# Four layers on one core: layer 1's mixing takes each token's second expert result by a product of its own

## The chip, the core and the metric

The kernel runs on one core of a Trainium2 chip. The core has five engines that work side by side, each with its own queue of instructions in order: TensorE (PE; PEld is its loading of stationary operands), VectorE (DVE), ScalarE (ACT), GpSimd (POOL) and SyncE (SP). SP issues most DMA transfers, POOL those whose rows are picked by an index (gathers). The metric is the device time of one execution in microseconds (us); lower is better.

## The reference, cut to what matters

The input is 32 sequences of 64 tokens, 2,048 tokens of 512 numbers. Four layers follow one another, and each adds to its input: `x = x + ffn(cond(x))`. Layer 0 ends in a mixture of 7 experts, of which each token uses 2; layer 1 begins with a mixing and goes on to a mixture of 32 experts, of which each token uses 4:

```python
x = x + _L0_ffn_ref(_L0_cond_ref(x, ...), ...)
x = x + _L1_ffn_ref(_L1_cond_ref(x, itok_B_0_7, L1_cond_weights), ...)

def _L1_cond_ref(x, subjects, weights):
    w = weights[subjects]
    out = jnp.einsum('bct,bcd->bdt', x, w)
    return out
```

For each of the 32 sequences the mixing picks one of 8 matrices of 64 by 64 and multiplies the 64 rows of the sequence by it. The input of this mixing is layer 0's result. For one token that is a sum: what layer 0 had before its routed experts, plus gate 0 times the result of its first expert, plus gate 1 times that of its second. The same sum is also the residual to which layer 1's result is added later.

## The kernel before, in words

Tokens are handled in 16 tiles of 128 (`NT`); a tile holds two sequences. All values are float32, and the program runs a float32 product as two passes of PE.

Both mixtures are worked by one class, `Moe`. In a loop over the tiles it scores the experts of each token and gives every pair of token and expert a slot: 640 slots for each of layer 0's experts and 320 for each of layer 1's. `Moe.put` does this slot arithmetic for groups of 4, 4, 4, 2, 1 and 1 tiles, on DVE with small products on PE (`at`, `tok`). `Moe.run` then goes through the slots: it gathers the tokens' rows from DRAM (`xr`, five tiles of 128 for a pair of units), turns them on PE (`tp`, copied out by ACT and DVE in turn as `xT`), multiplies by the gate and up weights (`gu`, L943, four buffers), applies the activation (for layer 1 `ga` on DVE, `sg` on ACT, `ga` times `sg` on POOL, `up` and `hT` on DVE, L671 to L678), multiplies by the down weights (`y`, L962), and stores the result (`yo`) in a DRAM array `ys`. A unit is 320 slots, which for layer 1 is one expert; each expert brings 1.5 MB of weights (`wt`, three buffers), loaded through SP's queue. After each tile of 128 results, `run` calls a function that it was given (`per_tile`), so that other work can be issued beside the experts.

`Moe.run` returns `combined`, which the next layer uses to fetch a tile of tokens: for each of a token's `K` experts it gathers the result from `ys` by its slot (`g.gather`, L284, on POOL) and adds it, times its gate, on DVE (L1010).

Layer 1's mixing (in `layer1`, L1090 to L1113) is the loop that the change touches. `Bridge` has prepared, beside layer 0's experts, the 16 tiles of x without the routed experts (`bridge.x`) and for each tile a 128x128 matrix `bridge.weights[i]` with the two sequences' matrices on its diagonal. For each tile the loop calls `combined` with `K0 = 2`, so two gathers and two adds, and stores the sum to the DRAM array `xs` (named `x1`), from which layer 2 will read it. Then comes one product with the mixing matrix (`mm`, L1094), a copy to SBUF by ACT (`c`), a store of the rows that the experts will gather, four transpositions (`tp`, L1100), another copy by ACT (`cT`), eight passes for the router's scores (`rp`, L1105), and on DVE the choice of the four best experts, with `m.put` for every finished group. When the loop is done, the slot lists are complete (`stok`, L792), and the first gathers of `Moe.run` can be issued.

A scheduler sets the order of each engine's instructions when the program is built, from the order in which they are written and its own estimates of cost; instructions marked as kept in program order stay where they are written. The order within a queue is then fixed, and an engine that waits holds back all that stands behind it. A tile pool gives each name its number of buffers (`bufs`): a writer waits until the last reader of the buffer is done. The pool `w2` holds the weights of layer 2, among them `mu` (`sb_mu`), 4 MB that are loaded beside layer 1's experts by the generator `layer2_ahead`; `layer1` calls it as `beside` from `ahead`, for every tile of results from the 17th on.

Of the kernel before, what the change touches and what calls it, by code (L numbers as in the profile page):

```python
# [9 lines left out]
F32 = mybir.dt.float32  # L10
# [4 lines left out]
AF = mybir.ActivationFunctionType  # L15
ALU = mybir.AluOpType
# [4 lines left out]
P = 128  # L21
B, T, D = 32, 64, 512
NT = B * T // P
# [5 lines left out]
E0, K0, C0, V0 = 7, 2, 640, 24  # L29
# [151 lines left out]
class Prog:  # L181
# [35 lines left out]
    def results(self, pool):  # L217

        zero = pool.tile([P, D], F32, name="zero")
        self.nc.vector.memset(zero, 0.0)  # L220
        self.ys = {}
        todo = []
        for E, C, V in ((E0, C0, V0), (E1, C1, V1)):
            t = self.dram.tile([E * C + V * P, D], F32, name=f"ys{E}")
            todo += [(t, r) for r in range(E * C, E * C + V * P, 8 * P)]
            self.ys[E] = t

        def step():
            if todo:
                t, r = todo.pop(0)  # L230
                self.dma(
                    t[r : r + 8 * P, :].rearrange("(v p) d -> p v d", p=P),
                    zero.unsqueeze(1).to_broadcast([P, 8, D]),
                )

        return step
# [444 lines left out]
class Moe:  # L681
# [228 lines left out]
    def run(self, xs, per_tile):  # L910

        g, nc, tc, E, K, C = self.g, self.g.nc, self.g.tc, self.E, self.K, self.C
        units = E * C // UNIT
        with ExitStack() as ctx:
            sb = ctx.enter_context(tc.tile_pool(name=f"es{E}", bufs=3, reuse_waits="tile"))
# [108 lines left out]
        def add(x, yk, gate):  # L1024
            g.pin(nc.vector.scalar_tensor_tensor(x, yk, gate, x, ALU.mult, ALU.add))

        combined.fetch = fetch
        return combined


# [42 lines left out]
def layer1(g, bridge, combined, beside, w2):  # L1073
    tc, nc, a = g.tc, g.nc, g.a
    with ExitStack() as ctx:
        keep = ctx.enter_context(tc.tile_pool(name="l1keep", bufs=1, reuse_waits="tile"))
        g.constants(keep, "cst01")
        xs = g.stream("x1")
        m = Moe(g, ctx, keep, E1, K1, C1, V1, "w_e1", W1R, l1_expert, None, bias="b_d1")
        with ExitStack() as c1:  # L1080
            wp = c1.enter_context(tc.tile_pool(name="l1w", bufs=1, reuse_waits="tile"))
            sb = c1.enter_context(tc.tile_pool(name="l1sb", bufs=3, reuse_waits="tile"))
            ps = c1.enter_context(tc.tile_pool(name="l1ps", bufs=2, space=PSUM, reuse_waits="tile"))
            wr = g.load(wp, "w_r1")
            br = g.load_bcast(wp, "b_r1")
            bank, at = (ps.tile([P, 512], F32, name=k, tag=k, bufs=1) for k in ("tok", "at"))
            m.begin(sb, bank, at)

            groups = {3: 4, 7: 4, 11: 4, 13: 2, 14: 1, 15: 1}
            for i in range(NT):  # L1090
                x = combined(sb, i, 3, bridge.x[i])
                nc.sync.dma_start(out=xs[i * P : (i + 1) * P, :], in_=x)
                o = ps.tile([P, D], F32, name="mm", tag="mm")
                nc.tensor.matmul(o, bridge.weights[i], x, start=True, stop=True)  # L1094
                c = sb.tile([P, D], F32, name="c")
                nc.scalar.copy(c, o)
                nc.sync.dma_start(out=m.rows[i * P : (i + 1) * P, :], in_=c)
                tp = ps.tile([P, 4, P], F32, name="tp", tag="tp")
                for cc in range(4):
                    nc.tensor.transpose(tp[:, cc, :], c[:, cc * P : (cc + 1) * P], g.ident)  # L1100
                cT = sb.tile([P, 4, P], F32, name="cT", bufs=2)
                nc.scalar.copy(cT, tp)
                rp = ps.tile([P, E1], F32, name="rp", tag="rp")
                for cc in range(4):
                    nc.tensor.matmul(rp, cT[:, cc, :], wr[:, cc, :], start=cc == 0, stop=cc == 3)  # L1105
                lg = sb.tile([P, E1], F32, name="lg")
                nc.vector.tensor_tensor(lg, rp, br, ALU.add)
                m.choose(i, lg)
                for last in (i - 1, i) if i == NT - 1 else (i - 1,):
                    if last in groups:  # L1110
                        m.put(sb, last + 1 - groups[last], groups[last])
            for e in range(2):
                m.weights(e)  # L1113
            m.end(sb)
            bridge.close()
        m.ready(ctx)

        gates, vals = m.gates, m.vals
        nc.vector.tensor_tensor(
            gates, vals[:, :, 0:K1], vals[:, :, 0:1].to_broadcast([P, NT, K1]), ALU.subtract  # L1120
        )
        nc.scalar.activation(gates, gates, AF.Exp)
        tot = keep.tile([P, NT], F32, name="tot1")
        nc.vector.tensor_reduce(tot, gates, AX.X, ALU.add)
        nc.vector.reciprocal(tot, tot)
        nc.vector.tensor_tensor(gates, gates, tot.unsqueeze(2).to_broadcast([P, NT, K1]), ALU.mult)

        def ahead(sb, ps, i):
            if i >= NT:
                w2["sb"], w2["ps"] = sb, ps  # L1130
                next(beside, None)

        combined = m.run(xs, ahead)
        m.beyond()
        return combined
# [975 lines left out]
def program(tc, a):  # L2111
    with ExitStack() as ctx:
        g = Prog(tc, a, ctx)
        w3 = {}
        pool3 = ctx.enter_context(tc.tile_pool(name="w3", bufs=1))
        bridge, combined = layer0(g, w3, pool3)
        first = ctx.enter_context(tc.tile_pool(name="w2a", bufs=1, reuse_waits="tile"))
        with tc.tile_pool(name="w2", bufs=1, reuse_waits="tile") as pool:
            w2 = {"pool": pool}
            beside = layer2_ahead(g, first, pool, w2)  # L2120
            combined = layer1(g, bridge, combined, beside, w2)
            for _ in beside:
                pass
            xs, xb = layer2(g, w2, combined, first, w3)
        layer3(g, w3, xs, xb)
# [17 lines left out]
```

## Time and profile before

| what | value |
|---|---|
| time, median of 3 runs | 2753.23 us (2749.45 to 2755.63) |
| the profiled execution, its own time | 2775.78 us |
| span of the profiled execution | 2774.0 us |
| busy over the span: PE, DVE, POOL, ACT | 2569.8, 1413.0, 845.6, 722.7 us |
| layer 1's mixing, from its first gather to the end of `stok` | 644.2 to 742.3 us |
| layer 1's experts, until PE's last product for them | 743 to about 1236 us |

The profile is one execution recorded by the hardware. Positions are microseconds from the start of the span. A row of a group names the line, the engine, the operation, what it writes and reads, the number of instructions, their busy time in us and the mean of one in ns, and behind the last bar the idle time of the engine before them with what ended it. A row in order of time begins with the start and the length in us; in square brackets stand the idle time before it and its releaser. The granted clock is the share of full speed at which PE ran.

### The profile page before, as it was taken

To read this page: it belongs to the slowest core of one execution; us is meant where nothing else is said; L and a number is where in the kernel's file an instruction comes from. 1 tells how busy PE (TensorE), PEld (TensorE's weight loads), DVE (VectorE), ACT (ScalarE), POOL (GpSimd) and SP (SyncE) were. 2 spreads that over 40 slices of the span, in tenths; PEclk is the share of its full clock that TensorE was granted. 3 is DMA by queue.
4 is the path that set the end of the run, shared out by engine and by line. 5 is a ranking of instruction groups with operands and counts; after the bars stand their busy time and mean duration, and the time that the engine had idled before them with its cause. 6 is when DMAs were issued, how large, how long until landed. Compare 5 with 4: busy or idle time off the path is not lost.

```text
span 2774.0 us, 41860 instructions
## 1 busy us (share of the span) xinstructions
PE 2569.8 (93%) x16508; PEld 1650.9 (60%) x16523; DVE 1413.0 (51%) x3439; ACT 722.7 (26%) x1501; POOL 845.6 (30%) x904
## 2 busy tenths in 40 slices
PE   6999989996799999978899999999999999887778
PEld 5777765564565565646666666776666654444444
DVE  4666655733644444435554444455544326555656
ACT  2444420011211121101222222222222212444444
POOL 2222215514223223212222221222222018655550
PEclk9999999996699999998999999999999999888889
DMA  2333215446557875643000000110001024233330
GB/s 95 128 128 128 86 55 178 137 164 216 191 182 251 321 258 197 220 144 115 28 28 28 27 28 28 36 46 27 28 27 51 9 97 154 71 90 97 98 98 29
DMA packets 111633, 299.50 MB, mean 108 GB/s; under 512 B 21177, under 2 KB 21977, under 8 KB 104128
## 3 DMA queue, kind: packets, MB, share of 16 engines
q1 hardware_dynamic: 75792, 201.78, 20.4%
q0 software_dynamic: 35056, 89.13, 10.8%
q10 hardware_dynamic: 576, 5.77, 0.5%
q8 instruction: 134, 2.20, 0.3%
q14 instruction: 75, 0.61, 0.1%
HBM read 225.08 MB, written 87.56 MB: 113 GB/s over the span
## 4 chain that ended last, share of the span: by engine, by line
PE 48%; DVE 2%; issue 2%; another core or an unknown queue 1%; DMA 1%; ACT 1%; POOL 0%; SPq 0%; ACTq 0%; POOLq 0%; DVEq 0%
PE lp L1376 8%; PE out L1519 8%; PE zp L1453 8%; PE pp L1833 3%; PE hp L1485 3%; PE gp L1508 2%; PE y L2080 2%; PE yp L1321 2%; PE op L2058 2%; PE sp L2011 2%; PE pT L2033 2%; PE ep L1462 1%; PE kp L1984 1%; PE ap L1309 1%
## 5 line engine op out<-in xcount | busy, mean ns | idle before, releaser
L943 PE MATMUL gu<-xT,wt 128*128 128x320 f32 x1472 | 408.7, 434 | 0.0
L943 PEld LDWEIGHTS gu<-xT,wt 128*128 128x128 f32 x1472 | 278.8, 191 | 123.4 <-issue 16.8
L1376 PEld LDWEIGHTS lp<-xnT,sb_mu 128*128 128x128 f32 x2048 | 236.2, 194 | 8.6 <-issue 6.7
L962 PE MATMUL y<-wt,hT 128*128 128x512 f32 (+1 forms) x552 | 240.3, 608 | 0.4 <-DVE yo L971 0.4
L1376 PE MATMUL lp<-xnT,sb_mu 128*128 128x128 f32 x2048 | 239.2, 277 | 1.5 <-DVE xnT L256 0.8
L1519 PE MATMUL out<-sb_w,gT 128*128 128x512 f32 x512 | 233.9, 599 | 0.0
L1453 PE MATMUL zp<-sb_w,xnT 128*128 128x512 f32 x512 | 226.5, 592 | 0.0
L1512 DVE COPY gT<-gp 128x512 f32<-128x512 f32 x64 | 44.3, 692 | 235.8 <-PE gp L1508 235.4
L1453 PEld LDWEIGHTS zp<-sb_w,xnT 128*128 128x128 f32 x512 | 93.7, 190 | 104.7 <-issue 100.9
L284 POOL DMA_INDIRECT xr<-rows,stok x115 | 110.0, 956 | 150.8 <-PE tp L924 78.7
L1519 PEld LDWEIGHTS out<-sb_w,gT 128*128 128x128 f32 x512 | 93.5, 190 | 103.7 <-issue 95.4
L284 POOL DMA_INDIRECT yk<-ys,slot x96 | 99.6, 1038 | 133.1 <-SPq L823 65.8
L962 PEld LDWEIGHTS y<-wt,hT 128*128 128x128 f32 (+1 forms) x552 | 80.4, 172 | 99.1 <-issue 83.2
L677 POOL TENSOR_TENSOR ga<-ga,sg 128x320 f32<-128x320 f32 x64 | 55.0, 859 | 267.5 <-ACT sg L673 263.9
L1530 POOL TENSOR_TENSOR xt<-xt,bc_bias 128x512 f32<-128x512 f32 x16 | 20.3, 1267 | 360.0 <-DMA x<-xt 360.0
L1490 ACT ACTIVATE h<-hp 128x512 f32<-128x512 f32 x128 | 69.5, 595 | 214.5 <-PE hp L1485 214.4
L284 POOL DMA_INDIRECT kvt<-kv,gidx x96 | 93.5, 973 | 102.2 <-PE op L2058 75.8
L2018 DVE CUSTOM_DVE_ANT_0 s<-sp,mask 128x336 f32<-128x336 f32 x128 | 61.2, 504 | 120.9 <-PE sp L2011 35.5
L1414 POOL TENSOR_TENSOR eT<-eT,inv 128x512 f32<-128x512 f32 x64 | 71.2, 1114 | 152.4 <-DVE inv L1413 151.4
L284 POOL DMA_INDIRECT kvt<-newkv,oidx x96 | 96.6, 1006 | 31.8 <-issue 29.2
L673 ACT ACTIVATE sg<-ga 128x320 f32<-128x320 f32 x64 | 30.0, 469 | 279.0 <-DVE ga L671 275.2
L924 PEld LDWEIGHTS tp<-sb_cst,xr 128*128 128x128 f32 x460 | 54.4, 148 | 67.2 <-issue 36.4
(379 smaller groups left out, 4647.7 us busy)
## 6 DMA issues: line engine op xcount, KB each, us to landing
wt<-w_e SPq DMA_DIRECT2D x32, 1538.0 KB
ys<-yo SPq DMA_DIRECT2D x115, 256.0 KB
ys<-zero SPq DMA_DIRECT2D x10, 2048.0 KB
xt<-x SPq DMA_DIRECT2D x62, 256.0 KB
x<-xt SPq DMA_DIRECT2D x48, 256.0 KB
wt<-w_e SPq DMA_DIRECT2D x7, 1536.0 KB
bd<-b_d SPq DMA_DIRECT2D x32, 256.0 KB
sb_w<-w SPq DMA_DIRECT2D x5, 1024.0 KB
```

What stands on the lines that cost most here:

```text
L284: ins = self.nc.gpsimd.indirect_dma_start(out=out, out_offset=None, in_=src, in_offset=bass.IndirectOffsetOnAxis(ap=idx, axis=0), **kw)
L943: nc.tensor.matmul(o, wj[:, c, ic * P : (ic + 1) * P], xT[:, c, :], start=c == 0, stop=c == 3)
L962: nc.tensor.matmul(y[row : row + n, :], hTs[u][:, ic, col : col + n], wd[:, ic, :], start=ic == 0, stop=ic == 1,)
L1321: g.first(c, nc.tensor.matmul(yp, self.xT[:, c, :], w["w_2"][:, c, :], start=c == 0, stop=False))
L1376: g.first(e + c, nc.tensor.matmul(lp[:, e, :], w["mu"][:, c, (4 * q + e) * P : (4 * q + e + 1) * P], self.xnT[:, c, :], start=c == 0, stop ...
L1414: g.pin(nc.gpsimd.tensor_tensor(e3, e3, inv.unsqueeze(2).to_broadcast([P, 8, T]), ALU.mult))
L1453: g.first(c, nc.tensor.matmul(zp, self.xnT[:, c, :], w["w1"][:, c, cols], start=c == 0, stop=c == 3))
L1485: g.first(e + b, nc.tensor.matmul(hp[:, b, e, :], self.ews[q][r, e, :], self.z[q][r, e * P : (e + 1) * P], start=True, stop=True))
L1490: g.pin(nc.scalar.activation(self.hs[q][b], hp[:, b], AF.Gelu))
L1519: g.first(e, nc.tensor.matmul(self.out, self.gTs[q][:, e, :], w["w2"][:, 4 * q + e, :], start=q + e == 0, stop=q + e == 6 and q == 3))
L1833: nc.tensor.matmul(pp, xT[i][:, c, :], (w["w_kv3"] if z else wq)[:, c, :], start=c == 0, stop=c == 3)
L2018: nc.vector.tensor_tensor_reduce(p, sps[j], self.masks[2 * i + half], -0.0625, 3.0e38, ALU.add, ALU.min, m)
```

## The change

The first result of each token is handled as before: gathered, multiplied by its gate and added to `bridge.x` on DVE. The product with the mixing matrix takes this partial sum. The second result is not added to it. Its rows are gathered (`y1of`) and are themselves the moving operand of a second product, whose stationary operand is the mixing matrix with row p multiplied by the gate of token p (`wbdg`, made by ACT). Both products accumulate in the same PSUM tile, so that the mixing sees the same sum as before. Nothing is rounded differently by type; all of it is float32.

The residual, which needs the whole sum, gets its second part later. The partial sums of all 16 tiles stay in SBUF (`x1in`, in the place that `sb_mu` takes afterwards). In `ahead`, beside the experts, for each of the first 16 tiles of results the second result of token tile `i` is gathered once more (two buffers), multiplied by its gate, added to `x1in` on DVE, and the sum is stored to `xs`. The stores to `xs` thus move from the mixing loop to the expert stage, and 16 gathers are added there; the mixing loop keeps its 32.

```diff
+        def result(pool, i, k, bufs):
+
+            yk = pool.tile([P, D], F32, name=f"y{k}of", bufs=bufs)
+            g.gather(yk, self.ys, self.slot[:, i, k : k + 1])
+            return yk, self.gates[:, i, k : k + 1]
+
+        combined.fetch, combined.result = fetch, result
@@ layer1
+        xk = w2["pool"].tile([P, NT, D], F32, name="x1in", tag="sb_mu")
+        results = combined.result
@@
             for i in range(NT):
-                x = combined(sb, i, 3, bridge.x[i])
-                nc.sync.dma_start(out=xs[i * P : (i + 1) * P, :], in_=x)
+                x, wbd = xk[:, i], bridge.weights[i]
                 o = ps.tile([P, D], F32, name="mm", tag="mm")
-                nc.tensor.matmul(o, bridge.weights[i], x, start=True, stop=True)
+                for k in range(K0):
+                    y, gate = results(sb, i, k, 3)
+                    if k == 0:
+                        nc.vector.scalar_tensor_tensor(x, y, gate, bridge.x[i], ALU.mult, ALU.add)
+                        nc.tensor.matmul(o, wbd, x, start=True, stop=False)
+                    else:
+
+                        wg = sb.tile([P, P], F32, name="wbdg", bufs=2)
+                        nc.scalar.activation(wg, wbd, AF.Copy, scale=gate)
+                        nc.tensor.matmul(o, wg, y, start=False, stop=True)
                 c = sb.tile([P, D], F32, name="c")
@@ ahead
             if i >= NT:
                 w2["sb"], w2["ps"] = sb, ps
                 next(beside, None)
+                return
+            y, gate = results(sb, i, 1, 2)
+            nc.vector.scalar_tensor_tensor(xk[:, i], y, gate, xk[:, i], ALU.mult, ALU.add)
+            nc.sync.dma_start(out=xs[i * P : (i + 1) * P, :], in_=xk[:, i])
```

More of the change, by code (lines that the diff above doesn't have):

```diff
@@ L1025, in add @@
             g.pin(nc.vector.scalar_tensor_tensor(x, yk, gate, x, ALU.mult, ALU.add))
-        combined.fetch = fetch
+        def result(pool, i, k, bufs):
[3 more added lines that the diff above has]
+        combined.fetch, combined.result = fetch, result
         return combined
```

## The prediction

> **What bounds the kernel now.** I read the page first, then stretches of 5 us around the edited loop, the groups of that loop, the rows in order of time where the next stage starts, and the waits of the expert stage. On the page: TensorE (PE) is busy 93% of the span, and its granted clock (PEclk, tenths, one digit per 69 us) falls to 6 only in slices 10 and 11, 624 to 763 us. That is where layer 1's mixing lies.
>
> ```profile
> PE 2569.8 (93%) x16508; PEld 1650.9 (60%) x16523; DVE 1413.0 (51%) x3439; ACT 722.7 (26%) x1501; POOL 845.6 (30%) x904
> ...
> PEclk9999999996699999998999999999999999888889
> ```
>
> Stretches of that stage (stretch, length, busy us of PE, PEld, DVE, ACT, POOL with instruction counts, granted clock, DMA share, GB/s):
>
> ```profile
> 655.00:660.00 5.00, 3.94 (x22) 2.78 (x21) 1.91 (x3) 1.76 (x4) 3.91 (x4) 0.84 0.95 285
> 660.00:665.00 5.00, 4.03 (x19) 3.06 (x20) 3.61 (x9) 1.75 (x3) 4.08 (x4) 0.84 0.94 315
> ...
> 675.00:680.00 5.00, 5.00 (x20) 3.97 (x19) 1.81 (x6) 1.75 (x3) 2.70 (x3) 0.50 0.96 311
> 680.00:685.00 5.00, 5.00 (x16) 3.50 (x16) 3.27 (x13) 0.98 (x2) 0.00 (x0) 0.50 0.37 131
> 685.00:690.00 5.00, 5.00 (x21) 4.00 (x20) 1.91 (x7) 1.74 (x4) 1.92 (x2) 0.50 0.53 186
> ...
> 705.00:710.00 5.00, 5.00 (x33) 3.53 (x32) 3.85 (x14) 3.23 (x6) 2.71 (x3) 1.00 0.99 320
> ```
>
> So the stage has three limits in turn: transfers until 680 (DMA share 0.95), then PE, busy without a gap from 675 to 695 but at half clock, then VectorE (DVE) with the slot arithmetic. Groups from 640 to 740 us:
>
> ```profile
> L284 POOL DMA_INDIRECT yk<-ys,slot x32 | 35.3, 1104 | 94.8 <-SPq L823 65.8 <-DVE vals L758 12.8 <-issue 7.6
> L1094 PE MATMUL mm<-xt,wbd 128*128 128x512 f32 x32 | 25.8, 902 | 17.1 <-DVE xt L1010 14.9 <-issue 1.6 <-DVE row L739 0.6
> L1010 DVE SCALAR_TENSOR_TENSOR xt<-yk,gates,xt 128x512 f32<-128x512 f32 x32 | 23.8, 745 | 16.0 <-DMA yk<-ys,slot 15.4 <-issue 0.5
> L1105 PE MATMUL rp<-sb_w_r,cT 128*128 128x32 f32 x128 | 23.0, 337 | 8.9 <-ACT cT L1102 6.8 <-DVE lg L1107 1.7 <-issue 0.5
> ```
>
> The experts follow. From 760 on PE is full, at clock 1.00, so any microsecond that it waits there lengthens the run. Rows at the seam (start, length, what):
>
> ```profile
> 743.10 0.94 POOL L284 DMA_INDIRECT xr<-rows,stok  x1 [34.57 <-DVE stok L792]
> ...
> 759.07 0.87 POOL L677 TENSOR_TENSOR ga<-ga,sg 128x320 f32<-128x320 f32 x1
> ```
> ```profile
> 746.51 1.09 PE L924 MATMUL tp<-sb_cst,xr 128*128 128x128 f32 x4 [4.67 <-DMA xr<-rows,stok]
> ...
> 776.67 1.09 PE L924 MATMUL tp<-sb_cst,xr 128*128 128x128 f32 x8
> ```
> ```profile
> 762.86 0.55 DVE L675 TENSOR_SCALAR up<-gu,wt 128x320 f32<-128x320 f32 x1 [1.15 <-PE gu L943]
> ...
> 775.84 0.69 DVE L256 COPY xT<-tp 128x512 f32<-128x512 f32 x1 [0.25 <-PE tp L924]
> ```
>
> A gather issued at 743.10 is used at 746.51: 3.4 us; the next four take 3.6 to 3.9, so I use 3.5. And the stage shows once what a held-up DVE does to PE, around 1045, where DVE waited for a POOL operation (waits, 1030 to 1055: us, times, longest):
>
> ```profile
> DVE cn L1174 <- POOL cn L308: 3.3, 1, 3.3
> ...
> PE tp L924 <- DVE xT L256: 2.4, 1, 2.4
> ```
>
> 3.3 us on DVE became 2.4 us of idle PE: the fourth turned tile of a pair needs the second one's evacuation by DVE.
>
> **The change, part by part. A: the mixing loop.** Gone: 16 of 32 adds of L1010 (16 x 0.745 = 11.9 us of DVE) and 16 stores of 256 KB, which leave SP's queue and a quarter of the loop's 64 transfers. Added: 16 products of two passes, and 16 small scalings on ScalarE (ACT). No row shows that scaling; ACT's 128x64 operation takes 0.26 us and its 128x320 copy 0.55, so 0.3 each, 4.8 in all, on an engine busy under 2 of 5 us in each stretch above: nothing, and 4.8 if that cover were gone. VectorE's add is no longer between the second gather and PE.
>
> The product is not small. Its two passes take 2.05 us at half clock (664.11) and 1.05 at full (666.81), the four transposes 1.06 and 0.60, the eight router passes 1.9 and 0.97. PE per tile: 5.0 (half) or 2.6 (full) before; 7.1 or 3.65 after. At full clock throughout: 16 x 3.65 = 58.4, plus the slot products (5.7 + 4.1 + 3.7 in the groups, at a mean clock near 0.65, so 8.8 at full) = 67.2. PE also waits once: in the built order DVE does three of the remaining adds between the first group's counting and the counts that PE needs, and their gathers, issued about 669 to 673 behind the earlier ones (1.25 us each), land 3.5 later: 3.1 us. The first product starts at 648.6 (landing 647.8, one add), so the last router product ends at 648.6 + 67.2 + 3.1 = 718.9 instead of 730.4: -11.5 us. The 12 us from there to the finished slot lists (742.35) are unchanged.
>
> What the clock does is not shown for this mix. In stretches of 1 us it falls at 670.3, in a wait of 5.3 us, and comes back at 704.2 only, though PE was nearly always busy between; it came back within 4 us where products and transposes ran back to back (650.3 to 656.3). The new sequence (product, transposes, product, then router passes) has 5.2 us of dense work in 7.1, the old one 3.1 in 5.0, so I expect it to recover in under 10 us, not in 31. I take one loss, at the 3.1 us wait: 9 us at half clock do 4.5 us too little. The row at 670.96 has ACT waiting 7.4 us for something remote while DMA share was 0.95; with fewer transfers I keep half, 3.7. A = -11.5 + 4.5 + 3.7 = about -3. Bounds: -11.5 (full clock, no such stall) and 2 x 67.2 + 3.1 - 81.8 = +56 (half throughout); at today's 0.65, 67.2/0.65 + 3.1 - 81.8 = +25. I stand nearest to the full-clock end, because of the dense rows.
>
> The Trainium skill, "TensorE: Matmul & The Clock Gate", Part 1, says that one busy window of about 3.4 us releases the clock; by it, A would be near -11.5. The rows speak against so simple a rule: 675 to 695, busy 5.00 of 5.00 at 0.50.
>
> **B: 16 gathers, adds and stores beside the experts.** All three go into queues that serve PE. In the built order POOL has the first two gathers behind ten gathers of rows, at 755.6 and 756.85, then pairs between its `ga` products; there are two buffers, so a gather waits for the add two before it. DVE has the adds in pairs between `ga`, `up` and `hT`, eleven of them ahead of the copies and clamps of the third unit. DVE runs in order, so each add that waits for a landing holds `up`, `yo` and `xT` behind it. One round of a pair: 3.5 landing + 0.75 add + 0.25 to the next issue = 4.5 us. Replayed: adds 0 and 1 fit (759.6, 760.9); gather 2 is issued at 762.75 behind `ga`, lands 766.25, add 2 ends 767.0, so `up` is at 767.0 instead of 762.86; add 4 ends 771.5, add 6 776.0, add 8 780.5, add 9 781.7; then `yo` 0.7, and `xT` ends at 783.1. PE does not miss `up` (`gu` has four buffers), but its fourth transposition, at 777.2 today (half of the row at 776.67), waits until 783.3: +6.1. A wait of that length cost the clock at 670.3; regained as at 751.6 to 755.3, 3.7 us at half: +2. Transfers beside it (stores of 256 KB, DMA share near 0.7 with gathers alone) add perhaps 0.3 to each of four rounds: +1. B = +9. Behind that, adds 11 to 15 find PE a unit ahead of need, and cost nothing.
>
> Bounds for B: landing would have to be 1.8 us to cost nothing, below any row, so the low end is 6.1 - 4 x 0.1 (landing 3.4), clock kept: +5.5; high: the slowest gather in the loop (issued 653.92, used 659.59: 5.7 us) makes four rounds 8.8 longer: +18.
>
> SP's queue: eleven stores now stand ahead of the fourth expert's weights. They would go at about 785 instead of 778.8 and take some 8 us (DMA is full from 780 to 787 today); PE wants them near 800: nothing, cover 6 us. The next weights stand behind store 15, about 800, where B has moved everything by 9 from 793.2 anyway: nothing. The tile that holds x shares its place with layer 2's `mu`, loaded only hundreds of us later: nothing.
>
> **Sum**: -3 + 9 = +6 us. The profiled execution took 2775.8 us (span 2774.0), 0.8% over the median 2753.2; the difference moves between them unscaled: 2782 there, 2759 as the time.
>
> **Rivals.** (1) Faster: the denser loop keeps the full clock. For it: the dense rows release the clock; against: the waits on landings. A = -11.5 and B at its low end give -6: 2747; it decides from a mean granted clock of 0.965 over the loop (67.2/0.965 + 3.1 = 72.7, 9 under 81.8). (2) The half clock stays: at 0.65, +25 + 9: 2787. For it: 31 us at 0.50 under full load; against: the router passes are a smaller share. (3) The expert stage hides the adds: -3, 2750. For it: DMA share is 0.01 from 765 to 770, so landings are quick; against: the 2.4 us at 1045. (4) Landings slow as in the loop: -3 + 18: 2768. For it: weights share the DMA engines.
>
> **How the numbers follow.** Chances: forecast 0.46, (1) 0.20, (2) 0.12, (3) 0.10, (4) 0.12. The forecast's own range, 2751 to 2769, comes from A between -8 and +5 and B between 6 and 12. The whole range goes to 2743 (both low ends, -6, and half of the stall that I kept) and 2781, most of the way to (2): 2 in 10 outside. 0.2%, 5.5 us, is about what a measurement here can tell from no change: faster 0.24 (1 and part of 3), same 0.26 (the rest of 3, and nearly half of the forecast), slower 0.50.
>
> **What would show it.** From the first gather to the first gather of expert rows: 95 us instead of 98.9, clock over 0.8. DVE's adds in the expert stage waiting for `y1of` for over 10 us in sum, in rounds of 4.5; PE's `tp` waiting for DVE `xT` for about 6 us near the second pair. I am wrong if that wait is absent, or the loop's clock is near 0.65 or 1.

## The result, and the profile after

The changed kernel took 2770.3 us (median of 6 runs, 2764.4 to 2771.6), the kernel before on the same chip 2752.3 (2747.4 to 2756.7): a ratio of 1.0056, 95% interval 1.0037 to 1.0074, so 10 to 20 us slower. The forecast was 2759, with 2751 to 2769 as its own range and 2743 to 2781 as the whole one: measured 1 us above the first, inside the second.

The two profiled executions alone would mislead: their spans are 2774.0 before and 2769.7 after. Before's lies 22 us above its timed median, after's inside its timed runs. So the two stages were measured one by one, and the kernel before was profiled twice more (runs e0 and e10 below). "Loop" is the time from the first gather of layer 1's mixing to the first gather of expert rows, "experts" from there to the end of the last `y` (in the first row at 1232.7):

| execution | loop us | clock 660 to 720 | experts us |
|---|---|---|---|
| before, as shown | 98.9 | 0.67 | 489.6 |
| before, second (e0) | 93.3 | 0.73 | 489.8 |
| before, third (e10) | 89.1 | 0.74 | 490.8 |
| after | 89.1 | 0.91 | 510.2 |

The expert stage repeats within 1.2 us, and the change lengthens it by 20. The loop of the same kernel differs by 10 us between the three profiles, and the one that I had read was the longest. The second and third come from two different chips (15 and 7; the chip of the first is not on record), so these three do not tell apart chip and execution. On chip 7 alone, 35 timed executions of this kernel spread over 16 us (2743.7 to 2760.0).

The page of the changed kernel:

```profile
PE 2564.8 (93%) x16555; PEld 1644.3 (59%) x16555; DVE 1415.8 (51%) x3439; ACT 727.3 (26%) x1517; POOL 863.6 (31%) x920
...
PEclk9999999998889999998999999999999999888889
```

Where before had 6 in slices 10 and 11, there are 8s now. Two stretches of the loop before, and then four of the changed loop (stretch, length, busy us of PE, PEld, DVE, ACT, POOL with instruction counts, granted clock, DMA share, GB/s):

```profile
660.00:680.00 20.00, 13.73 (x53) 10.18 (x53) 8.98 (x27) 5.26 (x9) 13.89 (x13) 0.67 0.94 318
680.00:700.00 20.00, 18.59 (x67) 14.12 (x67) 12.91 (x44) 4.70 (x9) 3.40 (x3) 0.50 0.37 125
```
```profile
640.00:660.00 20.00, 9.39 (x28) 4.58 (x28) 5.64 (x14) 2.36 (x5) 12.63 (x13) 0.69 0.61 173
660.00:680.00 20.00, 16.08 (x64) 9.91 (x64) 8.84 (x24) 5.82 (x13) 12.24 (x13) 0.83 0.74 224
680.00:700.00 20.00, 18.06 (x100) 11.95 (x100) 14.77 (x54) 9.42 (x20) 7.03 (x5) 0.91 0.45 142
700.00:725.00 25.00, 20.62 (x136) 14.41 (x135) 21.27 (x81) 10.38 (x21) 2.11 (x2) 0.92 0.56 202
```

From 660 to 680 the DMA share is 0.74 where it was 0.94, and from 660 on the clock stays at 0.83 to 0.92; before had 0.67 and 0.50 until 700. Groups from 640 to 740 us:

```profile
L1106 PE MATMUL mm<-x1in,wbd 128*128 128x512 f32 x32 | 20.4, 724 | 12.9 <-DVE x1in L1105 12.9
L1111 PE MATMUL mm<-y1of,wbdg 128*128 128x512 f32 x32 | 18.4, 660 | 0.0
L1122 PE MATMUL rp<-sb_w_r,cT 128*128 128x32 f32 x128 | 18.3, 290 | 7.7 <-issue 4.9 <-ACT cT L1119 2.8
...
L1110 ACT ACTIVATE wbdg<-wbd,gates 128x128 f32<-128x128 f32 x14 | 5.7, 406 | 0.0
```

PE has a second product of 18.4 us, and does its other work at a higher clock: a router pass (`rp`) is 290 ns instead of 337, the first product 724 instead of 902. PE never waits for the second product's operands.

In the expert stage PE's rows with a wait over 1 us, between 762 and 812 us (start, length, what, in brackets the idle time before and what ended it):

```profile
770.85 1.97 PE L962 MATMUL y<-wt,hT 128*64 128x512 f32 x2 [5.95 <-DVE yo L971]
775.03 1.12 PE L924 MATMUL tp<-sb_cst,xr 128*128 128x128 f32 x4 [1.17 <-DVE xT L256]
800.41 3.78 PE L962 MATMUL y<-wt,hT 128*128 128x512 f32 x4 [8.80 <-DVE yo L971]
```

And the stretches in which the clock was down for it, with two of the third execution of before behind them (columns as above):

```profile
770.00:775.00 5.00, 3.02 (x6) 1.01 (x6) 3.42 (x6) 0.59 (x1) 1.89 (x2) 0.50 0.84 279
775.00:780.00 5.00, 4.96 (x17) 2.71 (x18) 1.85 (x3) 0.59 (x1) 3.78 (x4) 0.62 0.97 277
...
800.00:805.00 5.00, 4.59 (x6) 2.19 (x7) 2.23 (x4) 0.00 (x0) 0.00 (x0) 0.50 0.28 105
805.00:810.00 5.00, 5.00 (x18) 3.46 (x17) 1.92 (x4) 0.47 (x1) 0.86 (x1) 0.89 0.95 304
```
```profile
770.00:775.00 5.00, 5.00 (x20) 3.52 (x19) 2.46 (x5) 0.53 (x2) 0.86 (x1) 1.00 0.98 400
...
800.00:805.00 5.00, 5.00 (x21) 3.50 (x20) 2.25 (x5) 0.74 (x2) 0.86 (x1) 1.00 0.98 399
```

The sum: PE waits 5.95 + 1.17 + 8.80 = 15.9 us that the third execution of before does not have (there PE is busy for 5.00 of 5.00 us at clock 1.00 in each stretch of 5 us from 760 to 815), and busy time at a lowered clock does 3.02 x 0.50 + 4.96 x 0.38 + 4.59 x 0.50 + 5.00 x 0.11 = 6.2 us too little. The first loss is 7.1 of waits and 3.4 of clock, the second 8.8 and 2.8. Together 22; the stage shows 20. What VectorE was doing at the two waits:

```profile
756.53 0.75 DVE L1151 SCALAR_TENSOR_TENSOR x1in<-y1of,gates,x1in 128x512 f32<-128x512 f32 x1 [3.50 <-DMA y1of<-ys,slot]
...
761.29 0.75 DVE L1151 SCALAR_TENSOR_TENSOR x1in<-y1of,gates,x1in 128x512 f32<-128x512 f32 x1 [1.56 <-DMA y1of<-ys,slot]
...
765.66 0.75 DVE L1151 SCALAR_TENSOR_TENSOR x1in<-y1of,gates,x1in 128x512 f32<-128x512 f32 x1 [0.26 <-DMA y1of<-ys,slot]
768.02 0.75 DVE L1151 SCALAR_TENSOR_TENSOR x1in<-y1of,gates,x1in 128x512 f32<-128x512 f32 x1 [1.61 <-DMA y1of<-ys,slot]
...
770.11 0.68 DVE L971 TENSOR_TENSOR yo<-y,bd 128x512 f32<-128x512 f32 x1
...
790.64 0.75 DVE L1151 SCALAR_TENSOR_TENSOR x1in<-y1of,gates,x1in 128x512 f32<-128x512 f32 x1 [8.89 <-DMA y1of<-ys,slot]
791.30 0.55 DVE L675 TENSOR_SCALAR up<-gu,wt 128x320 f32<-128x320 f32 x1
...
795.57 0.75 DVE L1151 SCALAR_TENSOR_TENSOR x1in<-y1of,gates,x1in 128x512 f32<-128x512 f32 x1 [1.74 <-DMA y1of<-ys,slot]
797.60 0.75 DVE L1151 SCALAR_TENSOR_TENSOR x1in<-y1of,gates,x1in 128x512 f32<-128x512 f32 x1 [1.28 <-DMA y1of<-ys,slot]
...
798.73 0.67 DVE L971 TENSOR_TENSOR yo<-y,bd 64x512 f32<-64x512 f32 x1
```

The first rounds of two gathers come 4.4 to 4.8 us apart, as forecast, and `yo` behind them starts 37.6 us after the first gather of rows (732.55), where before has it after 30.1 (773.18 from 743.10). The row at 790.64 was not forecast: the add of token tile 12 (add 12, counted from 0), whose gather was issued at 781.55, started 9.1 us later, and the clamp `up` behind it not before 791.30. Adds 14 and 15 waited once more, as POOL's next gather had stood 7.0 us for the buffer that add 12 held. Only then came the `yo` for which PE waited. From 780 to 790 the DMA share was 0.92 to 0.93. The transfers issued from 775 to 800, by kind:

```profile
wt<-w_e SPq DMA_DIRECT2D x1, 1538.0 KB
x<-x1in SPq DMA_DIRECT2D x6, 256.0 KB
...
xr<-rows,stok POOLq DMA_INDIRECT x5
y1of<-ys,slot POOLq DMA_INDIRECT x4
```

The weights went out at 778.10 and the five gathers of rows from 775.30 to 780.31, all ahead of the gather of 781.55. With 256 KB for each gather of rows these are 2.8 MB, 8 us at the 350 GB/s of that stretch (an estimate from above: part of it had landed by 781.55). That this queue of transfers made the landing slow is read from the order of issues; no run separates it.

### The profile page after: what moved, and what is told of

Its sections match the earlier page's. It is cut to its first block, busy times and chain, and to the rows that moved or that the text cites. A ratio compares the mean times of both kernels' runs of the same rounds, so it can differ in the third digit from the quotient of the medians.

```text
span 2769.7 us, 41967 instructions
## 1 busy us (share of the span) xinstructions
PE 2564.8 (93%) x16555; PEld 1644.3 (59%) x16555; DVE 1415.8 (51%) x3439; ACT 727.3 (26%) x1517; POOL 863.6 (31%) x920
## 4 chain that ended last, share of the span: by engine, by line
PE 48%; DVE 2%; issue 2%; another core or an unknown queue 1%; ACT 1%; DMA 1%; POOL 0%; SPq 0%; ACTq 0%; POOLq 0%; DVEq 0%
PE out L1540 8%; PE lp L1397 8%; PE zp L1474 8%; PE pp L1854 3%; PE hp L1506 3%; PE gp L1529 3%; PE yp L1342 2%; PE y L2101 2%; PE op L2079 2%; PE pT L2054 2%; PE sp L2032 2%; PE ep L1483 1%; PE kp L2005 1%; PE ap L1330 1%
## 5 line engine op out<-in xcount | busy, mean ns | idle before, releaser
L962 PE MATMUL y<-wt,hT 128*128 128x512 f32 (+1 forms) x552 | 243.1, 614 | 15.2 <-DVE yo L971 15.2
L1540 PEld LDWEIGHTS out<-sb_w,gT 128*128 128x128 f32 x512 | 93.3, 190 | 103.5 <-issue 95.2
L971 DVE TENSOR_TENSOR yo<-y,bd 128x512 f32<-128x512 f32 (+1 forms) x96 | 66.3, 690 | 50.1 <-PE y L962 45.8
```

The costliest lines, as they stand in the source:

```text
L962: nc.tensor.matmul(y[row : row + n, :], hTs[u][:, ic, col : col + n], wd[:, ic, :], start=ic == 0, stop=ic == 1,)
L971: nc.vector.tensor_tensor(yo[r], y[r], bd[r], ALU.add)
L1540: g.first(e, nc.tensor.matmul(self.out, self.gTs[q][:, e, :], w["w2"][:, 4 * q + e, :], start=q + e == 0, stop=q + e == 6 and q == 3))
```

## The experiments

The kernel before, two more times:

> The kernel before, unchanged: a second profile of it. The first profiled execution lasted 2775.8 us, 22 above the timed median, so the stage lengths taken from it (mixing loop 98.9 us from the first gather to the first gather of expert rows, experts 489.6 from there to the last product) may be long. If the 22 us lay elsewhere, both come out within 2 us of these. If they lay in these stages, the loop is shorter than 98.9 and the change gained less there than the 9.8 us that the two profiles show; the measured +18 against a stage sum of +10.5 would then be explained.

> The kernel before, unchanged, a third profile: the mixing loop took 98.9 and 93.3 us in the first two, the experts 489.6 and 489.8. I expect a loop between 90 and 99, experts within 1 us of 490: the executions differ in the loop. If it is at 89 or less, the changed loop gains nothing.

Measured: the table above; times 1.001 (0.9992 to 1.0029) and 1.0003 (0.9988 to 1.0019) of before. The loop's length in one profile is one draw out of a spread of at least 10 us. The third draw, 89.1, was expected at 90 to 99; it comes within 0.1 us of the point named there ("at 89 or less, the changed loop gains nothing"). A single pair of profiles can show no gain of 10 us in this loop.

**The loop alone (e1).** The gathers and adds beside the experts are left out, and with them the second results in the residual; the stores stay (`g.dma` keeps them in program order):

```diff
-            y, gate = results(sb, i, 1, 2)
-            nc.vector.scalar_tensor_tensor(xk[:, i], y, gate, xk[:, i], ALU.mult, ALU.add)
-            nc.sync.dma_start(out=xs[i * P : (i + 1) * P, :], in_=xk[:, i])
+            g.dma(xs[i * P : (i + 1) * P, :], xk[:, i])
```

> The change's mixing loop alone: two products per tile, and the partial sums stored beside the experts in program order, one behind each expert tile; no gather and no add there, so the second results are left out of the residual. My theory (the loop gains by the clock, the adds beside the experts cost by landings): loop 89 us, experts 490, time 2742, 10 under before. Rival, the stores beside the experts and not the adds are what costs: experts over 500, time over 2750. Rival, the loop's gain is given back by the next stage: loop 89, experts 500, time 2752.

Measured: loop 88.7 us at clock 0.89, experts 491.0, time 0.9988 of before (0.9969 to 1.0008), which is 3.3 us less, between 8.6 less and 2.2 more. The stores, kept in program order, cost nothing that the stage's spread shows. The gain of 10 us that I expected was worked out against the longest draw.

**The adds alone (e2).** The loop makes one product from the whole sum, and `xk` keeps the sum after the first add:

```diff
-                        nc.tensor.matmul(o, wbd, x, start=True, stop=False)
...
-                        nc.tensor.matmul(o, wg, y, start=False, stop=True)
+                nc.vector.scalar_tensor_tensor(bridge.x[i], y, gate, x, ALU.mult, ALU.add)
+                nc.tensor.matmul(o, wbd, bridge.x[i], start=True, stop=True)
```

> The gathers, adds and stores beside the experts alone, in the change's own order of instructions there; the mixing loop makes one product per tile from the whole sum, as before, with both adds, but without the 16 stores. My theory: experts 510 us (20 more than before), and the loop stays near 97, as its clock stays near 0.65 without the second product; time 2770. Rival, what the loop gained came from the 16 stores that left it and not from the second product: loop 89, time 2762. Rival, the cost beside the experts needs the changed loop in front of it: experts 490 to 500, time under 2755.

Measured: loop 91.8 at clock 0.76, experts 512.8, time 1.0065 (1.0042 to 1.0088), 18 us more. PE's and VectorE's waits in its expert stage (total us, times, longest), almost those of the change (15.2, 3, 8.8 and 24.7, 12, 8.9):

```profile
DVE x1in L1146 <- DMA y1of<-ys,slot: 22.9, 13, 9.2
PE y L962 <- DVE yo L971: 15.9, 3, 9.2
```

So the loss is whole without the changed loop in front of it. What the stores' leaving is worth in the loop can't be told: 91.8 lies within before's own draws.

**The adds later (e4).** Four buffers, and each add and store three expert tiles behind its gather, the adds held in program order (`g.pin`; the store that follows is not shown):

```diff
+            if i < NT:
+                held[i] = results(sb, i, 1, LAG + 1)
+            if i >= LAG:
+                j = i - LAG
+                y, gate = held.pop(j)
+                g.pin(nc.vector.scalar_tensor_tensor(xk[:, j], y, gate, xk[:, j], ALU.mult, ALU.add))
```

> The change, with each add and store put three expert tiles behind its gather (four buffers, adds held in program order): the same 16 gathers, adds and stores beside the experts, but a gather has some 15 us to land before DVE comes to its add. My theory (the cost beside the experts is DVE waiting for landings): experts 490 to 493 us instead of 510, time 2 to 4 us under the kernel before. Rival, the gathers' transfers and POOL's issues are what costs: experts 500 to 510, time 8 to 18 over the kernel before.

Measured: loop 90.2, experts 487.8, time 1.0007 (0.9998 to 1.0017). All 16 gathers, adds and stores are there, and the stage is as short as without them; the time is 2 us over before, where 2 to 4 under were expected. Of PE's waits there, those for VectorE's `yo` and `xT`:

```profile
PE y L962 <- DVE yo L971: 1.9, 2, 1.6
PE tp L924 <- DVE xT L256: 1.0, 2, 0.5
```

**Adds without gathers (e5).** The loop keeps the 16 second results (in the place of a weight that is loaded later), and the adds read them there, one per tile; adds and stores are held in program order (not shown):

```diff
+        yk = w2["pool"].tile([P, NT, D], F32, name="y1in", tag="sb_w1")
...
-            y, gate = results(sb, i, 1, 2)
+            y, gate = yk[:, i], combined0.gates[:, i, 1:2]
```

> The change without the second gathers: the mixing loop keeps the 16 second results in SBUF, and the adds beside the experts read them there, one behind each expert tile, with the stores. My theory: 16 adds of 0.75 us that wait for nothing fit into DVE's idle time, experts 490 to 492 us, time 2 to 4 under the kernel before. Rival, DVE's 12 us of adds are themselves what costs: experts 500 or more, time 6 or more over before.

Measured: experts 491.2, as expected: 12 us of adds, one behind each tile, fit into VectorE's idle time. But the time was 1.0024 (1.0012 to 1.0036), 6.4 us over before instead of 2 to 4 under. Its loop took 93.2, the longest of the changed loops. Whether that is its draw, or comes from gathers that no longer wait for buffers, is open.

**Gathers without adds (e6).** The tiles are gathered, nothing reads them, and the second results are missing from the residual; the stores are held in program order, as in e1:

```diff
             y, gate = results(sb, i, 1, 2)
-            nc.vector.scalar_tensor_tensor(xk[:, i], y, gate, xk[:, i], ALU.mult, ALU.add)
-            nc.sync.dma_start(out=xs[i * P : (i + 1) * P, :], in_=xk[:, i])
+            g.dma(xs[i * P : (i + 1) * P, :], xk[:, i])
```

> The change with the 16 gathers and stores beside the experts but no adds (the second results are left out of the residual; the gathered tiles are read by nothing). The gathers stand in POOL's queue nearly as in the change, two buffers, so they are held only by their own writes. My theory: experts 490 to 493 us, time 2 to 4 under before, since nothing on DVE waits for a landing. Rival, the transfers or POOL's issues in front of its own products hold PE: experts 500 to 510.

Measured: loop 88.9, experts 502.6, time 1.0079 (1.0051 to 1.0108). My theory in its narrow form, VectorE waiting for landings, falls: here no add waits, and 12.5 of the stage's 20 us are there. POOL's rows in order of time (start, length, what, idle time before and what ended it):

```profile
764.66 0.94 POOL L284 DMA_INDIRECT y1of<-ys,slot  x1 [0.79 <-DMA y1of<-ys,slot]
767.07 0.94 POOL L284 DMA_INDIRECT y1of<-ys,slot  x1 [1.46 <-DMA y1of<-ys,slot]
768.03 0.86 POOL L677 TENSOR_TENSOR ga<-ga,sg 128x320 f32<-128x320 f32 x1
...
777.95 0.94 POOL L284 DMA_INDIRECT y1of<-ys,slot  x1 [3.48 <-DMA y1of<-ys,slot]
```

VectorE, one view of the same stretch:

```profile
763.97 0.33 DVE L676 TENSOR_SCALAR up<-up 128x320 f32<-128x320 f32 x1
768.93 0.49 DVE L678 TENSOR_TENSOR hT<-up,ga 128x320 f32<-128x320 f32 x1 [4.63 <-POOL ga L677]
...
788.57 0.49 DVE L678 TENSOR_TENSOR hT<-up,ga 128x320 f32<-128x320 f32 x1 [6.83 <-POOL ga L677]
```

With two buffers a gather waits until the one two before it has landed. POOL too works in order: its product `ga` stands behind three or more such gathers, `hT` on VectorE waits for `ga` (21.6 us in sum), `yo` stands behind `hT`, and PE waits 7.9 us for `yo`. The same early place can do it on either engine's queue. In the change itself VectorE waits for `y1of` (24.7 us), and no wait of `hT` for `ga` stands in its list: the path of e6 is another one than that of the 20 us.

**Five buffers (e7).**

```diff
-            y, gate = results(sb, i, 1, 2)
+            y, gate = results(sb, i, 1, 5)
```

> The change with five buffers for the second results instead of two; the adds stand where they stood, early on DVE. My theory: a gather no longer waits for the add two before it, so the rounds of 4.5 us for two become issues of 1.25 us each; the last adds come some 10 to 12 us sooner and the landing behind the held-up weights goes: experts 497 to 503 us, time 3 to 9 over before. Rival, the landings themselves are slow because of the transfers beside them, whatever the buffers: experts 508 to 512, time 15 over before.

Measured: loop 86.6, experts 499.0, time 1.0050 (1.0032 to 1.0067). The stage is where the theory had it: half the loss. One wait of PE for `yo` is left (7.3 us), the second is gone. So at this early place the two buffers are half of the loss. The time is 13 us over before, though, not 3 to 9.

**Adds held in program order (e9).** One word around the add, every other line as in the change. In the built order the gathers move too: between 762 and 783 POOL issues four of them, where the change issues eight.

```diff
-            nc.vector.scalar_tensor_tensor(xk[:, i], y, gate, xk[:, i], ALU.mult, ALU.add)
+            g.pin(nc.vector.scalar_tensor_tensor(xk[:, i], y, gate, xk[:, i], ALU.mult, ALU.add))
```

> The change with one difference: each add beside the experts is held at its place in program order, behind its own expert tile, so that adds no longer stand in front of the third unit's clamps and copies; still two buffers, and the gathers follow wherever a buffer comes free. My theory (it is the early place in VectorE's and POOL's queues that costs, not the work): experts 488 to 492 us, time 5 under to 2 over before. Rival, two buffers are too few and each add still meets its landing: experts 500 or more, time 8 or more over before.

Measured: loop 88.1, experts 491.9, time 0.9996 (0.9982 to 1.0010). Its waits in the expert stage:

```profile
POOL y1of L284 <- DVE x1in L1151: 29.5, 11, 5.6
DVE x1in L1151 <- DMA y1of<-ys,slot: 11.5, 4, 4.0
...
PE y L962 <- DVE yo L971: 1.6, 2, 0.9
```

POOL and VectorE still wait, 41 us in sum, but one gather and one add per tile leave PE a margin: 1.6 us of waits for `yo` instead of 15.2, and clock 1.00 from 760 to 815. With e4 this settles the cause: the place of the gathers and adds in the first units' queues. The same work and the same transfers cost nothing clear of noise in a later place, and there two buffers are enough. Which part of the loss is the adds' place and which the gathers', e9 does not tell, as both moved.

**One product twice (e8),** in the loop of the kernel before:

```diff
-                nc.tensor.matmul(o, bridge.weights[i], x, start=True, stop=True)
+                for _ in range(2):
+                    nc.tensor.matmul(o, bridge.weights[i], x, start=True, stop=True)
```

> The kernel before, with its one mixing product made twice per tile (the second overwrites the first with the same values): PE gets the change's 16 further products, while VectorE's adds and the stores stay. By busy time alone the loop grows by 16 products, 16.8 us at full clock and 32.8 at half: over 110 us, time 17 or more over before. My theory (the denser sequence holds the clock, and PE has room while the loop waits for results): the loop stays between 90 and 100 us with a clock over 0.7 from 660 to 720, time within 6 us of before.

Measured: loop 93.6, experts 489.7, time 1.0028 (1.0014 to 1.0041), 7.7 us more (3.9 to 11.3). Stretch 660 to 720 of the third execution of before, and then of this kernel (columns as above):

```profile
660.00:720.00 60.00, 46.10 (x250) 33.16 (x250) 47.40 (x155) 20.84 (x39) 20.81 (x19) 0.74 0.67 229
```
```profile
660.00:720.00 60.00, 52.00 (x270) 33.21 (x268) 43.03 (x134) 19.89 (x36) 21.85 (x21) 0.86 0.67 228
```

With more work for PE the granted clock is 0.86, where it is 0.67 to 0.74 in three executions of before and 0.76 in e2, which also makes one product per tile; the nine profiles of the changed loop, with two products, have 0.83 to 0.95. Of the 16.8 us of full-clock products about half came out as time. The loop itself, 93.6, lies within before's draws. My bound of 6 us was a little low; 17 or more is excluded.

**The second result added in the loop (e3, e11),** behind the second product, from the tile that this product reads; only the stores go beside the experts:

```diff
                         nc.tensor.matmul(o, wg, y, start=False, stop=True)
+                        nc.vector.scalar_tensor_tensor(x, y, gate, x, ALU.mult, ALU.add)
```

> The change with the second result added in the mixing loop, from the tile that the second product reads, behind that product and with no second gather; only the stores go beside the experts, in program order. My theory: loop 90 to 92 us (DVE has its 16 adds back, but PE does not wait for them), experts 490, time 2744, faster than both kernels. Rival, the 16 adds of 0.75 us on DVE hold back the first results' adds as before: loop 97 to 99, time 2752. Rival, the stores cost beside the experts: experts 500, time 2755.

> The version with the second result added in the mixing loop behind its product and only the stores beside the experts, again, with more executions: 0.10% under before in the first comparison, interval 0.28% under to 0.07% over. My theory: the loop's 4 us are real, 0.1 to 0.2% under before. Rival: no difference, a ratio of 1.000.

Measured: loops of 89.1 and 88.8 us at clock 0.95 and 0.94, experts 489.5 and 488.2, times 0.9990 (0.9972 to 1.0007) and 1.0018 (1.0005 to 1.0031). The two comparisons straddle no change, and the theory of e11, 0.1 to 0.2% under before, falls. No version here beats the kernel before; those with the loss removed (e3, e4, e9, e11) equal it within 0.2%.

## Why the prediction was right or wrong, point by point

**Right in its sign, its range and in most of its parts; too small in one term.** By stages the change is about -5 (mean of before's three loops, 93.8, against 88.6, the mean of the six profiles that have the change's loop unaltered: after, e1, e4, e6, e7, e9) and +20: about +15 to the measured +15.4 (ratio times 2752; 18.0 between the medians). The agreement is closer than the -5 deserves, which rests on three draws that lie 10 us apart.

- **Base.** The loop's 98.9 us were taken as a property of the kernel; they were the longest of three draws. This step failed and did no harm by luck: the changed loop was put at 95 and measured 88.6 in the mean, 6 too long, and the loop before was 5 too long, so the difference held.
- **A = -3.** In time e1 has -3.3 (-8.6 to +2.2), which fits and also holds zero; e11, with a loop as short (88.8) and only stores beside the experts, is 5 us over before (1.4 to 8.5). So a gain in time is not shown, and the parts of A can't be told one by one. The full-clock bound of -11.5 did not come, though the clock was 0.91 and about half of the loop ran at 1.00: after its first product PE still waits, 8.7 us for VectorE's slot arithmetic, 2.8 for ACT's `cT` and 4.9 for nothing that the profile names. The Trainium skill's rule that the prediction weighs ("TensorE: Matmul & The Clock Gate", Part 1: one busy window of about 3.4 us releases the clock) is nearer to this loop than to before's, where PE was busy for 20 us at 0.50. No run settles what keeps the clock down.
- **Clock over 0.8, recovery in under 10 us; a stage of 95 us.** 0.91 measured, and no stay below 1.00 between 655 and 720 was over 10 us; the stage was 89.1, in a spread of 86.6 to 90.2.
- **ACT's scaling at nothing.** 0.406 us each, not 0.3, and PE never waited for it: right.
- **B, the first wait: +6.1 on `tp` for `xT`.** PE waited 5.95 for `yo` and then 1.17 for `xT`, 7.1 in all. Rounds of 4.5: 4.4 to 4.8. The chain was right; the copy `yo`, one place further up on VectorE, was met first.
- **"Adds 11 to 15 find PE a unit ahead of need, and cost nothing": this step failed.** Forecast at nothing, this second loss measured 11.6 us (8.8 of waits and 2.8 of clock), more than the first (10.5, forecast at 9). Add 12's gather landed after 9 us, not 3.5 (nor the 5.7 of the upper bound), and PE waited 8.8 us for `yo`. I had the third expert's weights, the gathers of rows and the stores each in the text, but costed each queue for itself and not the landing of a gather issued behind all of them.
- **Clock in B: +2.** Two losses, 6.2 us.
- **B's upper bound, +18,** was worked out from four slow rounds; it is 2 under the 20 measured, from another mechanism. Rival (4), 2768, came nearest in time, in part by luck: one landing was slow, at 9 us, not four rounds at 5.7.
- **SP's queue at nothing.** Five stores held SP from 780.37 to 798.69, and the next expert's weights went out at 804.23 instead of 781.61 (third execution of before). No wait of PE for weights followed: right.
- **POOL's queue** was in the text only as the place of gathers. That `ga` behind waiting gathers is a second path to the same loss was not seen; e6 shows it at +12 to +13 us for the stage.
- **Slips in the working, none of which moves the forecast.** B's low end is 5.7 by its own terms (6.1 - 4 x 0.1), not 5.5, and the whole range's low end 2745, not 2743. ACT is busy 3.23 of 5 us in the last stretch shown, not under 2. The gather issued at 748.10 is used after 4.6 us, not 3.6 to 3.9, though PE had other work until then. The clock came back 6 us after 650.3, not within 4.

What stays open: the times of e4 to e7 stand 2 to 10 us further above before than their stages do (against the shortest draw of before). These ran on a chip from which no profile of before was taken, but that is not the whole of it: e11 has the same gap, 8 us, against the profile of before from its own chip (e10). Its profiled execution took 2747.2 us, 9 under its own median, so one profile does not stand for the median.

## What to carry to other kernels

Work moved "beside" a stage costs by where its instructions stand in the in-order queues there, not by its size: 16 gathers and adds cost 20 us in front of the first units' clamps and copies, and nothing clear of noise when one add stood behind each tile. Where a compiler or scheduler sets that order, look at the built order of every engine that the moved work touches, the one that issues the gathers too. And before a stage's length is used as a base, profile the kernel more than once: here the same stage took 89 to 99 us in three profiles.

## What the runs showed of the hardware that was not expected

- The same kernel before took 2752, 2763, 2753 and, on one chip, 2664 us (medians). On that chip the clock granted from 2500 to 2660 us was 1.00 (in e4 to e7), where all other profiles have 0.83 to 0.91. Only ratios within one chip compare.
- A gather of 256 KB took 3.4 us from issue to use at the start of the expert stage (DMA share 0.48 from 743 to 749) and 9 us behind a load of weights and five other gathers (0.92 to 0.93). No run shows which of these transfers made it slow.
- With more products in a loop that waits, the granted clock was higher: 0.86 (e8) after 0.67 to 0.74. The 16 products cost 7.7 us, not the 16.8 of their full-clock busy time; how much of that is the clock, and how much idle time that they filled, no run separates.
